# A graph network's edge lists, late node tiles and last normalizings, put in another order

## The chip, the cores and the metric

The kernel runs on one core of a Trainium2 chip. The metric is the device time of one execution in microseconds (us). The engines named below are TensorE (PE, its weight loads PEld), VectorE (DVE), ScalarE (ACT), GpSimd (POOL) and SyncE (SP). "SPq", "ACTq" and the like are the DMA queues that an engine issues to. L12 is line 12 of the kernel before.

## The reference, cut to what matters

There are 12,500 nodes of 128 features and 400,000 edges, sorted by destination.

```python
rbf = exp(-(distances[:, None] - centers) ** 2 / (2.0 * width * width))       # 50 centers, 0 to 10
cut = 0.5 * (cos(pi * distances / 10.0) + 1.0) * (distances <= 10.0)
W = (silu(rbf @ fw1 + fb1) @ fw2 + fb2) * cut[:, None]
messages = (h[src] @ pw + pb) * W
agg = segment_sum(messages, dst, 12500)
gnn = h + (silu(agg @ mw1 + mb1) @ mw2 + mb2)
x = layernorm(x + gnn)                                                        # h is x
```

Distances are drawn up to some 56, so most edges lie past the cutoff of 10 and add nothing.

## The kernel before, in words

**Edges.** Edges past the cutoff are dropped on the chip. The edge list is taken in seven chunks. For each, `load_rows` brings lengths, sources and destinations into SBUF, and `pack(c)` (L693) moves the edges that stay together: passes of shifts on DVE, by one, two, four places and so on (L515, L519, L509), then places within the whole from sums on PE (L729, read by DVE at L503), then a scatter to DRAM (`packed`) that GpSimd issues. `unpack(c)` (L811) reads the packed list back: loads of three lists by SP (L821), merged by DVE (`one_of`, L839 and L840, and two more operations to L869), transposed by PE (L902, in `to_places`, L899) and copied by DVE (L907) into `srci` (the source of each edge, by which rows are gathered). Between the transposes and that copy stands `lengths`, a merge of the edge lengths and their stores by SP. Then the same for `dl` (place within a window of destinations) and `cut` (the cutoff's factor); `at_row` (L921) holds addresses for rows that are copied singly.

The packed edges make 139 quads (`NL`) of 512 edges, four to each partition. The third chunk (c = 2) holds quads 24 to 45.

**A planner's order.** `pack` and `unpack` are generators: each `yield` gives the estimated time of what was recorded, and adds to an estimated clock. `pack_until` takes the next step of the first chunk whose due time `awake[c]` is not ahead of that clock; a chunk whose loaded lists haven't been taken into use (`c in sent`) goes first. `awake[c]` is set where a step has to wait for something: after the list's loads (L831) and, by `later`, between PE's transposes and the copies behind them (L906). The order in which instructions are recorded is the order in which each engine runs them, so a due time moves DVE, PE, SP and GpSimd work against the quads' work. The gathers (`fetch`) are recorded as far ahead as the lists are known and buffers are free.

**Quads.** For each quad q the main loop (L1489 to L1550) records:

- `fetch`: four indirect gathers on GpSimd (L1048), one row of `proj` (x @ pw + pb) for each partition. For eight quads the first of the four is replaced by single rows that SP copies. Each gather also waits for a sum some quads back (`FOLLOW`, "keeps pace with the sums"; L1051).
- `radial`, `basis`, `first`, `silu`, for two quads at a time: lengths by DMA, Square and Exp on ACT (L1094, L1095), PE by fw1 (L1103), Silu on ACT (L1109). `second`: PE adds fb2 (L1117) and multiplies by fw2 (L1120).
- `message`: DVE multiplies by the gathered rows (L1131); `place`: DVE makes the columns that hold cut at the destination's place (L1143); `sum_up`: PE sums over the edges (L1163) into one or two windows of destinations; `add`: DVE adds these to `aggT` (L1196).

Exp, Silu and the root (Sqrt) stand in different tables of ACT; a change from one to the other shows as ACT_TABLE_LOAD.

**Nodes.** From quad 70 on, `nodes(q)` (L1296) and `tail(q)` (L1337) take blocks of node tiles (128 nodes each) as their sums are complete: `node_first` (L1200; PE at L1204 and L1205, Silu on ACT), `node_second` (PE), `node_stats` (L1219; residual and statistics on DVE), `deviations` (L1232; four small operations on DVE, the last at L1240, and the root on ACT, L1241), `scales` (L1244; reciprocal at L1248 and L1249 on DVE), `normalize` (L1255; ACT at L1263, or DVE at L1260, then the store, L173). The early blocks, of four tiles, have one root for four blocks. The late ones begin at tiles 80 (4 tiles), 84 (4), 88 (2), 90 (3), 93 (2) and 95 (3, behind the last quad).

What touches the change near the end: the roots of the last early blocks and of tile 80 are recorded at quads 133 and 132 (`nodes` and L1532, `NL` - 6 and `NL` - 7), the latter followed by a Silu of one element (`warm`), which loads silu's table again. The last pair of quads' `silu` is recorded at quad 133 behind the first of these. At quad 133 `tail` records `keep_busy(8)` (L1342), eight products on PE into the bank `ph` that serve nothing (L1352), ahead of `node_first(84)`. Two more of them stand at each of the last quads (L1510). At the end, behind the last quad, stand `deviations([95])` and then the normalizings of tiles 90 to 92, 93 and 94 on ACT, `scales` of 95 to 97, and their normalizing, two on DVE and one on ACT.

```python
1051            if table is None and idx is None and len(last_sum) > FOLLOW:
1052                tc.add_manual_dep(ins.ins, last_sum[-1 - FOLLOW], mybir.DependencyInfo(
```

Of the kernel before, what the change touches and what calls it, by code (L numbers as in the profile page):

```python
# [43 lines left out]
NL = 139  # L44
# [39 lines left out]
def kernel(  # L84
# [37 lines left out]
    nc = tc.nc  # L122
# [215 lines left out]
    srci = keep.tile([P, NP, 2], I32, name="srci")  # L338
# [61 lines left out]
    clock = [3.2]  # L400
# [3 lines left out]
    awake = [0.0] * NC_  # L404
# [406 lines left out]
    def unpack(c):  # L811
# [15 lines left out]
        if c < 2:  # L827
            more_ = np_ if c == 0 else SPILL
            also = work.tile([P, 2, QE], F32, name="s", bufs=3).bitcast(I32)
            listed(also, 0, more_, 3, LISTS)  # L830
        awake[c] = max(awake[c], clock[0]) + (6 if c < 1 else 3.5 if c < 2 else 4.0)  # L831
        yield 0
        def alike_in(k):
            nc.vector.tensor_tensor(pair[:more_, :LISTS - 3, k::2], pair[:more_, :LISTS - 3, k::2],
# [46 lines left out]
        def later(more=0.0):  # L881

            if c or known[0] >= DIRECT // QT:
                awake[c] = clock[0] + (5.0 if known[0] >= QB[c + 1] else 1.0 if c == 0 else 2.5) + more
                return 0.0
            return 0.5
# [12 lines left out]
        def to_places(f, to):  # L899
            t, tp = turned()  # L900
            for j in range(2):
                nc.tensor.transpose(tp[:, j, :np_], f[:, j * P:(j + 1) * P], ident[:np_, :np_])  # L902
            if to is srci:
                lengths()
                yield 1.4 if c < 2 else 0.8
            yield later(-2.0 if c == 1 and to is srci else 0.0)  # L906
            nc.vector.tensor_copy(to[:, p0:p0 + np_, :].rearrange("p r j -> p j r"),  # L907
                                  tp[:, :, :np_])
            back(t)
# [288 lines left out]
    zs_of, py_of, st_of = {}, {}, {}  # L1198
# [20 lines left out]
    def node_stats(t0, st, between=lambda: None):  # L1219

        r = rows(t0)
        y, b = x_sb[t0], py_of.pop(t0)
        py = b.rearrange("p (k f) -> p k f", k=4)
        for a, c, m in alike(r):
            nc.vector.scalar_tensor_tensor(y[:m, a:a + c], y[:m, a:a + c], 2.0, py[:m, a:a + c],
                                           op0=OP.mult, op1=OP.add)
        free.append(b)
        between()
        for k, m in enumerate(r):
            nc.vector.bn_stats(st[:m, k, :], y[:m, k, :])  # L1230
# [13 lines left out]
    def scales(group, both, s):  # L1244

        n = s.shape[1]
        r, by = (work.tile([P, 16], F32, name=k, bufs=2)[:, :n] for k in ("rs", "by"))
        nc.vector.reciprocal(r, s)  # L1248
        nc.vector.scalar_tensor_tensor(by, both[:, :, 0], -0.5, r, op0=OP.mult, op1=OP.mult)  # L1249
        at = 0  # L1250
        for t in group:
            ready.append((t, r[:, at:], by[:, at:]))
            at += len(rows(t))

    def normalize(t0, rs, by, on=(), eng=nc.sync):  # L1255

        y = x_sb.pop(t0)
        for k, m in enumerate(rows(t0)):
            if k in on:
                nc.vector.tensor_scalar(y[:m, k, :], y[:m, k, :], rs[:m, k:k + 1], by[:m, k:k + 1],  # L1260
                                        op0=OP.mult, op1=OP.add)
            else:
                nc.scalar.activation(y[:m, k, :], y[:m, k, :], AF.Identity, bias=by[:m, k:k + 1],  # L1263
                                     scale=rs[:m, k:k + 1])
        node_dma(t0, y, out, True, eng=eng)

    ready = []
# [18 lines left out]
    begin, at_q = {}, NODES  # L1286
# [4 lines left out]
        begin[t0] = [at_q, at_q + 1, at_q + (4 if NODES + 24 < at_q < NL - 20 else 3)]  # L1291
        at_q += 2 if at_q % 4 == 1 else 3
    early = list(begin)
    assert begin[early[-1]][2] <= NL - 3

    def nodes(q):  # L1296

        if deep:
            scales(*deep.pop())
        for _ in ready[:1 if q < NL - 6 else 2]:  # L1300
            normalize(*ready.pop(0))
        for k, t0 in enumerate(early):
            if begin[t0][0] - 5 == q:
                load_x(t0)
            if begin[t0][2] == q:
                if k % 4 == 0:
                    st_of[0] = statistics()
                node_stats(t0, st_of[0][:, k % 4 * 4:])
                if k % 4 == 3:
                    deep.append(deviations(early[k // 4 * 4:k + 1], st_of[0]))  # L1310
            if begin[t0][1] == q:
                node_second(t0)
            if begin[t0][0] == q:
                node_first(t0)
        for k, t0 in enumerate(TAIL):
            if q == NL - 9 + k:
                load_x(t0)
        if q == NL - 7:
            st_of[3] = statistics()
            node_stats(80, st_of[3])  # L1320
        if q == NL - 4:
            node_stats(84, st_of[3][:, 4:])
        if q == NL - 3:
            node_stats(88, st_of[3][:, 8:])
            dev_of.append(deviations([84, 88], st_of[3][:, 4:]))
            nc.scalar.activation(warm, half_pi, AF.Silu)
        if q == NL - 2:
            node_second(90)
            for k in (1, 2):
                st_of[k] = statistics()  # L1330
            scales(*dev_of.pop(0))
            for _ in (84, 88):
                normalize(*ready.pop(0))
# [3 lines left out]
    def tail(q):  # L1337

        for t0, k in READY.items():
            if q == NL - k:  # L1340
                if t0 == 84:
                    keep_busy(8)  # L1342
                assert done_to(2 * added(q + 1)) >= (t0 + TAIL[t0]) * P
                node_first(t0)
            if q == NL - k + 1 and t0 in (80, 84, 88):
                node_second(t0)

    def keep_busy(n):

        ph = ps.tile([P, 2, QE], F32, name="ph", bufs=1)  # L1350
        for k in range(n):
            nc.tensor.matmul(ph[:, k % 2, :], ones_b[:, :P],  # L1352
                             bias_b["mb2"].rearrange("k j f -> k (j f)"), start=True, stop=True)
# [135 lines left out]
    for q in range(NL - 1):  # L1489
        while todo and q + 2 >= DIRECT // QT and todo[0] <= chunk_of(min(q + 2, NQ - 1)):  # L1490
            go_on(todo[0])
        msg = message(q)
        if q == NL - 2:
            bases_of(q, NL)
        nodes(q)
        most[0] = room(q)
        fetches(clock[0], most[0])
        fetches(math.inf, min(NL, q + AHEAD + 1))
        assert fetched[0] > QT * min(NL - 1, q + AHEAD)
        if q >= CLEAR_Q:  # L1500
            clear()
        if loads_later and q >= 8:
            nc.sync.dma_start(*loads_later.pop(0))
        radials(q // 2 + 5)
        one_by_one()
        multiplies(q + 1 + EARLY_X)
        if q + 2 < NL:
            second(q + 2)
        if q % 4 < 2 and 2 * octs(q) < NL:
            first(octs(q))  # L1510
            silu(octs(q))
        if q % 4 == 3:
            for o in (q // 4 * 2 + 4, q // 4 * 2 + 5):
                if 2 * o < NL:
                    basis(o)
        if q > NL - 5:
            keep_busy(2)
        sum_up(q, msg)
        now = range(added(q), added(q + 1))
        for k in now if q < NL - 2 else ():  # L1520
            base_of(k, (0,))
        if q < NL - 2:
            place(q + 1)
        if q == NL - 4:
            place(NL - 1)
        if q == NL - 2:
            for j in range(QT):
                sum_up(NL - 1, message(NL - 1, (j, j + 1)), (j,))
        for k in now:
            if q < NL - 2:  # L1530
                base_of(k, (1,))
            if q == NL - 7 and k == now[0]:  # L1532
                deep.append(deviations([80], st_of[3]))
                nc.scalar.activation(warm, half_pi, AF.Silu)
            add(k)
        tail(q)
        clock[0] = max(clock[0], there_at[q])
        summed[q] = clock[0] + 0.7
        clock[0] += 2.2 + 0.3 * (windows(q) - 1)
        if q == 0:  # L1540
            clear_packed(2, nc.sync)
        if todo:
            pack_until(max(there_at[q + 1], clock[0] + (PACK_US if known[0] >= QB[3] else EARLY_US)), NC_)
        if NODES - 8 <= q < NODES - 2:
            part_of(*(("mb1", mb1_f) if q < NODES - 5 else ("mb2", mb2_f)), (q - NODES + 8) % 3)
        if not todo and not counted:
            counted.append(q)
            count()
        elif counted and some is None and fetched[0] >= QT * NL:
            some = nc.values_load(bad_i[0:1, 2:3], min_val=0, max_val=3 * E)  # L1550
# [9 lines left out]
    node_second(95)  # L1560
    early_dev = deviations([90, 93], st_of[1])
    node_stats(95, st_of[2], lambda: scales(*early_dev))
    last_dev = deviations([95], st_of[2])
    for _ in (90, 93):
        normalize(*ready.pop(0))
    scales(*last_dev)
    normalize(*ready.pop(0), on=(0, 1), eng=nc.scalar)

# [110 lines left out]
```

## Time and profile before

| | |
|---|---|
| time, median of 3 runs | 734.89 us (734.77 to 734.94) |
| the profiled execution | 736.03 us |
| its span in the trace | 734.3 us |
| granted clock of PE, mean | 0.92 |
| PE busy | 590.7 us (80%) |
| DVE busy | 560.2 us (76%) |
| GpSimd busy | 533.5 us (73%) |
| ACT busy | 403.0 us (55%) |
| DMA, mean | 124 GB/s |

A line of the page's groups or of the trace's views names the line of the kernel, the engine, the operation, and output <- inputs by the program's names, with the shapes. "x3" is the number of instructions. A bracket gives the engine's idle time ahead of the instruction and what released it. A name can be that of another use of the same buffer, since buffers are shared: a message may be called `msg` or `quad`. The granted clock is the share of full speed that PE was allowed.

### The profile page before, as it was taken

The numbers are of one execution on the slowest core, as the hardware profiler recorded it, in microseconds if no ns is written. First come the engines' busy times: TensorE is split into PE (matmuls) and PEld (weight loads), VectorE is DVE, ScalarE is ACT, GpSimd is POOL, SyncE is SP. The second block draws the span as 40 slices with busy tenths as digits, with TensorE's granted clock in tenths as the row PEclk, the third lists the DMA queues.
The fourth block names the chain that finished last, engine by engine and source line by source line (L and its number), as shares of the span: only waits on it lengthen the run. The fifth ranks groups of instructions, "written<-read, shape, count | busy, mean of one in ns | idle before, by whom it ended". The sixth has DMA issues, their size and how long they took to land.

```text
span 734.3 us, 13663 instructions
## 1 busy us (share of the span) xinstructions
PE 590.7 (80%) x3527; PEld 461.9 (63%) x3527; DVE 560.2 (76%) x1737; ACT 403.0 (55%) x574; POOL 533.5 (73%) x569
## 2 busy tenths in 40 slices
PE   6877876797888787878698969999978787778684
PEld 5766565676666665667476758777656565565463
DVE  8899798878878997989889957877455555556663
ACT  6557634274444864536457256859456644653763
POOL 7777777577777777777777777777777777777750
PEclk9999687999999998989989989999998999999886
DMA  8995442233234323343233343535333433343231
GB/s 267 313 318 189 143 128 73 89 120 99 76 110 128 95 85 101 99 127 88 83 111 113 96 134 97 155 120 151 110 113 94 127 124 98 98 142 116 79 114 53
DMA packets 53103, 91.37 MB, mean 124 GB/s; under 512 B 13824, under 2 KB 20576, under 8 KB 53018
## 3 DMA queue, kind: packets, MB, share of 16 engines
q1 hardware_dynamic: 34466, 53.20, 21.8%
q0 software_dynamic: 17840, 36.77, 18.1%
q8 instruction: 29, 0.48, 0.3%
q10 hardware_dynamic: 712, 0.46, 0.2%
q14 instruction: 56, 0.46, 0.2%
HBM read 74.59 MB, written 15.79 MB: 123 GB/s over the span
## 4 chain that ended last, share of the span: by engine, by line
DMA 13%; PE 13%; DVE 11%; POOL 9%; issue 6%; ACT 3%; DVEq 1%; POOLq 0%; SPq 0%; ACTq 0%
DMA quad<-proj,srci 11%; POOL quad L1048 9%; PE ph L1103 3%; PE bank L1120 3%; PE sums L1163 3%; DVE hot L1143 2%; DVE quad L1143 2%; PE bank L1205 1%; DVE msg L1131 1%; DMA pair<-packed 1%; DVE aggT L1196 1%; DVE st L1230 1%; DVEq L1173 1%; ACT x L1263 1%; DMA packed<-line,at_i 1%
## 5 line engine op out<-in xcount | busy, mean ns | idle before, releaser
L1048 POOL DMA_INDIRECT quad<-proj,srci x421 | 400.9, 952 | 132.5 <-issue 94.9
L1120 PEld LDWEIGHTS bank<-fw_sb,s 128*128 128x128 f32 x1112 | 159.7, 207 | 72.9 <-issue 65.8
L1109 ACT ACTIVATE s<-ph 128x1024 f32<-128x1024 f32 x70 | 71.2, 1017 | 179.7 <-PE ph L1103 179.5
L1120 PE MATMUL bank<-fw_sb,s 128*128 128x128 f32 x1112 | 159.7, 291 | 0.0
L1103 PE MATMUL ph<-rbf,w_sb 102*128 102x512 f32 x278 | 145.9, 651 | 6.7 <-ACT s L1109 3.5
L1163 PEld LDWEIGHTS sums<-hot,msg 128*128 128x128 f32 x816 | 107.6, 198 | 55.9 <-issue 27.5
L1143 DVE TENSOR_SCALAR hot<-iota_n,dl,cut 128x80 f32<-128x80 f32 (+4 forms) x408 | 109.1, 341 | 27.5 <-PE sums L1163 25.3
L1163 PE MATMUL sums<-hot,msg 128*128 128x80 f32 (+4 forms) x816 | 110.4, 280 | 14.2 <-DVE msg L1131 13.9
L1117 PE MATMUL bank<-fb_b,ones_b 96*128 96x512 bf16 x139 | 56.5, 406 | 54.8 <-DVE msg L1131 34.1
L1048 POOL DMA_INDIRECT x<-proj,srci x79 | 75.5, 955 | 24.2 <-issue 19.8
L1131 DVE TENSOR_TENSOR msg<-bank,quad 128x512 f32<-128x512 f32 (+1 forms) x82 | 55.5, 677 | 45.9 <-DMA quad<-proj,srci 41.6
L1103 PEld LDWEIGHTS ph<-rbf,w_sb 102*128 102x128 f32 x278 | 52.6, 211 | 46.1 <-issue 38.3
L1196 DVE TENSOR_TENSOR aggT<-aggT,sums 128x80 f32 (+4 forms) x209 | 53.9, 258 | 32.4 <-PE sums L1163 11.1
L1094 ACT ACTIVATE rbf<-d,rbf_bias,rbf_scale 102x512 f32<-102x512 f32 x70 | 56.3, 804 | 19.6 <-DMA d<-near_d 19.6
L1048 POOL DMA_INDIRECT quad<-in_x_dram,srci x48 | 46.7, 974 | 15.7 <-issue 11.9
L334 PEld LDWEIGHTS bank<-pw_sb,xT 128*128 128x128 f32 (+1 forms) x292 | 43.0, 212 | 9.4 <-issue 6.0
L1109 ACT ACT_TABLE_LOAD x36 | 46.2, 1283 | 0.6
L1095 ACT ACT_TABLE_LOAD x35 | 44.9, 1283 | 0.6
L1095 ACT ACTIVATE rbf<-rbf 102x512 f32<-102x512 f32 x70 | 44.1, 630 | 1.5
L334 PE MATMUL bank<-pw_sb,xT 128*128 128x128 f32 (+1 forms) x292 | 43.3, 296 | 0.7 <-ACT xT L984 0.6
L1163 PE MATMUL sums<-quad,quad 128*128 128x128 f32 (+3 forms) x296 | 40.8, 284 | 2.9 <-DVE quad L1131 2.8
L1143 DVE TENSOR_SCALAR quad<-iota_n,dl,cut 128x128 f32<-128x128 f32 (+3 forms) x148 | 40.6, 353 | 3.3 <-issue 2.1
(272 smaller groups left out, 791.4 us busy)
## 6 DMA issues: line engine op xcount, KB each, us to landing
d<-near_d SPq DMA_DIRECT2D x70, 256.0 KB
dl<-proj SPq DMA_DIRECT2D x1024, 0.5 KB
x<-in_x_dram SPq DMA_DIRECT2D x46, 256.0 KB
quad<-proj,srci POOLq DMA_INDIRECT x421
proj<-hp SPq DMA_DIRECT2D x24, 256.0 KB
out_dram<-x SPq DMA_DIRECT2D x22, 256.0 KB
r_d<-in_edge_weight_dram SPq DMA_DIRECT2D x5, 256.0 KB
r_dst<-in_dst_dram SPq DMA_DIRECT2D x5, 256.0 KB
```

Of the source, the lines that this page charges most:

```text
L334: nc.tensor.matmul(to[:m, k, :], lT[:, k * P:k * P + m], w, start=False, stop=(k == a + c - 1))
L1048: ins = nc.gpsimd.indirect_dma_start(out=got[:, j, :], out_offset=None, in_=proj if table is None else table, in_offset=bass.IndirectOffse ...
L1094: nc.scalar.activation(rbf[:u], d[:u], AF.Square, bias=rbf_bias[:u], scale=rbf_scale[:u])
L1095: nc.scalar.activation(rbf[:u], rbf[:u], AF.Exp, scale=-1.0 / (2.0 * width * width))
L1103: nc.tensor.matmul(ph[:, h, :], w1_sb[:2 * KR, h, :], rbf[:2 * KR], start=True, stop=True)
L1109: nc.scalar.activation(s[:, :n], ph[:, :n], AF.Silu)
L1117: nc.tensor.matmul(pu, ones_b[:, :P], bias_b["fb2"].rearrange("k j f -> k (j f)"), start=True, stop=False)
L1120: nc.tensor.matmul(pu[:, j * H:(j + 1) * H], s[:, j * P:(j + 1) * P], fw2_sb, start=False, stop=(j == QT - 1))
L1131: nc.vector.tensor_mul(msg[:, a:b, :], pu_of[q].rearrange("p (j f) -> p j f", j=QT)[:, a:b, :], got_of[q][:, a:b, :])
L1143: nc.vector.tensor_scalar(hot[:, j, :wide(q)], iota_n[:, :wide(q)], dl[:, at[0], at[1]], cut[:, at[0], at[1]], op0=OP.is_equal, op1=OP.mult)
L1163: ins = nc.tensor.matmul(pa[:, k * W:k * W + wide(q)], msg[:, j, :], hot[:, j, :wide(q)], start=(j % n == 0), stop=(j % n == n - 1))
L1196: nc.vector.tensor_add(to, to, pa[:, k * W:k * W + wide(q)])
```

## The change

It has three parts.

1. The third chunk's lists. After their loads (L831) the due time of chunk 2 is set to the estimated clock itself instead of 4.0 us later, and the copy of its `srci` (L906) is due 2.5 us sooner behind PE's transposes. The merges are thus recorded right behind the loads.
2. The late roots. The root of the last early blocks is not recorded in `nodes` at quad 133 any more, but within that quad's additions (L1532), directly ahead of tile 80's, which moves there from quad 132; both stand behind the last `silu` of the quads. `nodes` takes all waiting groups in `scales` at quad 134, the older first. The eight fillers ahead of `node_first(84)` go. An assertion now says that the last early block ends at quad 133.
3. The end. `normalize` takes an argument for the engine of its first kind of normalizing. Tiles 90 to 92 are normalized on GpSimd, 93 and 94 on ACT, and both are recorded ahead of the last root, `deviations([95])`.

```diff
--- before.py
+++ after.py
@@ -828,7 +828,7 @@
             more_ = np_ if c == 0 else SPILL
             also = work.tile([P, 2, QE], F32, name="s", bufs=3).bitcast(I32)
             listed(also, 0, more_, 3, LISTS)
-        awake[c] = max(awake[c], clock[0]) + (6 if c < 1 else 3.5 if c < 2 else 4.0)
+        awake[c] = max(awake[c], clock[0]) + (6 if c < 1 else 3.5 if c < 2 else 0.0 if c < 3 else 4.0)
         yield 0
         def alike_in(k):
             nc.vector.tensor_tensor(pair[:more_, :LISTS - 3, k::2], pair[:more_, :LISTS - 3, k::2],
@@ -903,7 +903,7 @@
             if to is srci:
                 lengths()
                 yield 1.4 if c < 2 else 0.8
-            yield later(-2.0 if c == 1 and to is srci else 0.0)
+            yield later((0.0, -2.0, -2.5, *4 * (0.0,))[c] if to is srci else 0.0)
             nc.vector.tensor_copy(to[:, p0:p0 + np_, :].rearrange("p r j -> p j r"),
                                   tp[:, :, :np_])
             back(t)
@@ -1252,12 +1252,12 @@
             ready.append((t, r[:, at:], by[:, at:]))
             at += len(rows(t))
 
-    def normalize(t0, rs, by, on=(), eng=nc.sync):
+    def normalize(t0, rs, by, on=(), eng=nc.sync, v=nc.vector):
 
         y = x_sb.pop(t0)
         for k, m in enumerate(rows(t0)):
             if k in on:
-                nc.vector.tensor_scalar(y[:m, k, :], y[:m, k, :], rs[:m, k:k + 1], by[:m, k:k + 1],
+                v.tensor_scalar(y[:m, k, :], y[:m, k, :], rs[:m, k:k + 1], by[:m, k:k + 1],
                                         op0=OP.mult, op1=OP.add)
             else:
                 nc.scalar.activation(y[:m, k, :], y[:m, k, :], AF.Identity, bias=by[:m, k:k + 1],
@@ -1291,12 +1291,12 @@
         begin[t0] = [at_q, at_q + 1, at_q + (4 if NODES + 24 < at_q < NL - 20 else 3)]
         at_q += 2 if at_q % 4 == 1 else 3
     early = list(begin)
-    assert begin[early[-1]][2] <= NL - 3
+    assert begin[early[-1]][2] == NL - 6
 
     def nodes(q):
 
-        if deep:
-            scales(*deep.pop())
+        while deep:
+            scales(*deep.pop(0))
         for _ in ready[:1 if q < NL - 6 else 2]:
             normalize(*ready.pop(0))
         for k, t0 in enumerate(early):
@@ -1306,7 +1306,7 @@
                 if k % 4 == 0:
                     st_of[0] = statistics()
                 node_stats(t0, st_of[0][:, k % 4 * 4:])
-                if k % 4 == 3:
+                if k % 4 == 3 and q != NL - 6:
                     deep.append(deviations(early[k // 4 * 4:k + 1], st_of[0]))
             if begin[t0][1] == q:
                 node_second(t0)
@@ -1338,8 +1338,6 @@
 
         for t0, k in READY.items():
             if q == NL - k:
-                if t0 == 84:
-                    keep_busy(8)
                 assert done_to(2 * added(q + 1)) >= (t0 + TAIL[t0]) * P
                 node_first(t0)
             if q == NL - k + 1 and t0 in (80, 84, 88):
@@ -1529,7 +1527,8 @@
         for k in now:
             if q < NL - 2:
                 base_of(k, (1,))
-            if q == NL - 7 and k == now[0]:
+            if q == NL - 6 and k == now[0]:
+                deep.append(deviations(early[-4:], st_of[0]))
                 deep.append(deviations([80], st_of[3]))
                 nc.scalar.activation(warm, half_pi, AF.Silu)
             add(k)
@@ -1560,9 +1559,9 @@
     node_second(95)
     early_dev = deviations([90, 93], st_of[1])
     node_stats(95, st_of[2], lambda: scales(*early_dev))
+    normalize(*ready.pop(0), on=(0, 1, 2), v=nc.gpsimd)
+    normalize(*ready.pop(0))
     last_dev = deviations([95], st_of[2])
-    for _ in (90, 93):
-        normalize(*ready.pop(0))
     scales(*last_dev)
     normalize(*ready.pop(0), on=(0, 1), eng=nc.scalar)
```

## The prediction

> **What bounds the kernel now.** I read the page's groups first, then GpSimd's timeline, then the chain of waits, then the other engines where GpSimd stands.
>
> ```profile
> L1131 DVE TENSOR_TENSOR msg<-bank,quad 128x512 f32<-128x512 f32 (+1 forms) x82 | 55.5, 677 | 45.9 <-DMA quad<-proj,srci 41.6
> ```
>
> Behind the first bar stand busy time, mean ns of one, and the idle time before, with what ended most of it: VectorE's messages (L1131) wait above all for gathered rows. GpSimd gathers them (L1048), four gathers to a quad of 512 edges. In the timeline (start, length, and in brackets the idle time before and its releaser) one takes 0.95 us and the next starts 0.30 us later, so a quad costs 5.0 us. They stand back to back but for one hole, just ahead of quad 24, the first whose rows the third chunk's lists name:
>
> ```profile
> 130.54 1.00 POOL L1048 DMA_INDIRECT quad<-proj,srci  x1 [0.30 <-issue]
> 135.96 0.94 POOL L1048 DMA_INDIRECT quad<-proj,srci  x1 [4.42 <-DVE at_row L921]
> ...
> 680.02 0.94 POOL L1048 DMA_INDIRECT quad<-proj,srci  x1 [0.30 <-issue]
> ...
> 708.85 0.95 POOL L1048 DMA_INDIRECT quad<-proj,srci  x1 [0.30 <-issue]
> ```
>
> The last releaser named is at_row, but the built program has gather 24 wait for the copy of srci (L907), which starts at 135.44 and is the instruction ahead of at_row. The hole is worth 4.42 - 0.30 = 4.12 us.
>
> Does GpSimd set the end? The chain of waits holds this piece (start, length), the landing of quad 132's last gather:
>
> ```profile
> 680.02 2.48 DMA quad<-proj,srci
> ```
>
> So a gather lands 2.48 us after its start, and here the chain waits for that. Early on the gathers lead: near 130 GpSimd is at quad 24 and DVE (rows below) at message 5; near 488 it is at quad 94 and DVE at message 90, which is the least lead there is, and from then on messages wait for rows. At the end it is otherwise: the last gather, started at 708.85, lands at 711.33, yet the last message (below) starts only at 715.16. There the other engines are late. So two stages count: the hole near 131, if its gain survives to 488, and the stretch from 682 to the end.
>
> **Part 1, the third chunk's lists.** What stands now:
>
> ```profile
> 116.57 0.77 SPq L821 DMA_DIRECT2D pair<-packed  x2
> ...
> 200.43 0.79 SPq L821 DMA_DIRECT2D pair<-packed  x2
> ```
> ```profile
> 120.20 0.68 DVE L515 TENSOR_SCALAR bank<-nodes 128x512 int32<-128x512 int32 x1
> 125.27 0.22 DVE L503 TENSOR_SCALAR at_f<-bank,end 128x1 f32<-128x1 f32 x1 [2.28 <-PE bank L729]
> 127.73 0.67 DVE L1131 TENSOR_TENSOR msg<-bank,quad 128x512 f32<-128x512 f32 x1
> 129.87 0.41 DVE L839 TENSOR_TENSOR two<-pair 44x256 int32<-44x256 int32 x1
> 135.44 0.25 DVE L907 CAST srci<-bank 128x88 int32<-128x88 f32 x1 [0.43 <-PE bank L902]
> 204.34 0.42 DVE L839 TENSOR_TENSOR two<-pair 46x256 int32<-46x256 int32 x1 [0.53 <-DMA pair<-packed]
> ```
> ```profile
> 124.79 0.36 PE L729 MATMUL bank<-run,ones 128*128 128x1 f32 x2
> 156.75 1.00 PE L1163 MATMUL sums<-hot,msg 128*128 128x56 f32 x8
> ```
>
> In the new order the merge (L839 to L869, four operations, 1.5 us) stands right behind the L515 of 120.20, so at 120.9. Are the lists there? The next chunk's load was issued at 200.43 and its merge, which waited for it, ran at 204.34: 3.9 us. So this one is there at 120.5, 0.4 us ahead. Then come the rest of the first shifting pass (L519 and two L509, 2.0 us) and the lengths (0.85 us), to 125.2. PE's transposes (L902) now stand right behind the L729 of 124.79 and end near 125.4; the copy of srci ends near 125.9. Gather 24 may then start at 130.54 + 1.00 + 0.30 = 131.84, and the hole is gone: **-4.12 us**, bounds 0 and -4.4 (the whole idle time).
>
> What is behind the new waits: the message of quad 5 stands behind that copy at 125.6, 2.1 us ahead of its 127.73, since the wait of 2.28 us for L729 falls away (at_f now comes later). No arithmetic is added. SP's stores of the lengths and the row loads of single quads move with the list, the stores earlier by some 7 us; nothing but DVE's merge waits on SP here.
>
> What is late next? The built program lets each gather also wait for a sum (L1163) four quads back by the order of recording, and in the new order quads 24 to 33 wait for a sum one later. The tightest is the second gather of quad 28, the 17th behind that of 135.96 and so at 157.21 (17 x 1.25): it waits for sum 9, the row of 156.75, which ended at 157.75. Without the hole it comes to start at 153.1. If the sum did not move, the whole gain would be lost there. It does move: two whole passes of the fourth chunk's shifting (four operations of 0.7 us as that of 120.20, 2.8 us each) now stand behind message 9 instead of ahead of it. With 5.6 us less DVE work and 2.3 us less waiting ahead of it, against 1.5 to 3 us of new waits of DVE for sums (two buffers of one-hot columns turn round), sum 9 ends 4.9 to 6.5 us earlier, 151.2 to 152.9 by an estimate from these rows. It fits, with 0.2 to 1.9 us to spare.
>
> The next narrow place is where the lead runs out:
>
> ```profile
> 488.38 0.95 POOL L1048 DMA_INDIRECT quad<-proj,srci  x1 [0.32 <-issue]
> ```
> ```profile
> 436.07 0.42 DVE L839 TENSOR_TENSOR two<-pair 54x256 int32<-54x256 int32 x1 [7.17 <-DMA dl<-proj]
> 486.93 0.69 DVE L1131 TENSOR_TENSOR quad<-bank,quad 128x512 f32<-128x512 f32 x1
> ```
>
> Quad 94 is gathered into the buffer that message 90 reads until 487.62, 0.76 us before the gather's start. With GpSimd 4.12 us ahead, message 90 must come 3.4 us earlier. It can: ahead of it DVE stands 7.17 us for the last chunk's lists, and the new order puts that merge behind message 79 instead of 77. Its scatter, one quad of gathers later but 4.12 us ahead, gives the lists at 436.07 + 5.0 - 4.12 = 436.95; two messages are then done during the wait, which puts message 80 where 78 was, plus 0.9 us. That is some 7 us earlier from there on. So I keep 4.12.
>
> **Part 2, both roots behind the last silu, no fillers.**
>
> ```profile
> 687.44 1.28 ACT L1241 ACT_TABLE_LOAD   x1
> 693.72 1.28 ACT L1109 ACT_TABLE_LOAD   x1
> 695.02 0.60 ACT L1109 ACTIVATE s<-ph 128x512 f32<-128x512 f32 x1
> 711.88 1.28 ACT L1241 ACT_TABLE_LOAD   x1 [2.82 <-DVE v L1240]
> ```
> ```profile
> 689.07 0.18 DVE L1248 RECIPROCAL rs<-dev 128x4 f32<-128x4 f32 x1 [1.00 <-ACT dev L1241]
> 692.86 0.61 DVE L1196 TENSOR_TENSOR aggT<-aggT,sums 128x128 f32 x2
> 715.16 0.88 DVE L1131 TENSOR_TENSOR quad<-bank,quad 128x128 f32<-128x128 f32 x4
> ```
> ```profile
> 695.66 3.57 PE L1352 MATMUL ph<-mb_b,ones_b 96*128 96x512 bf16 x8 [5.54 <-ACT s L1109]
> 699.46 1.91 PE L1205 MATMUL bank<-aggT,mw_sb 128*128 128x512 f32 x2
> 702.86 1.06 PE L1163 MATMUL sums<-quad,quad 128*128 128x128 f32 x8
> 713.75 0.91 PE L1205 MATMUL bank<-aggT,mw_sb 128*128 128x384 f32 x2 [1.95 <-DVE aggT L1196]
> 718.91 1.31 PE L1163 MATMUL sums<-quad,quad 128*128 128x128 f32 x8
> ```
>
> Now ACT loads the root's table (687.44), silu's, the root's again and silu's (693.72), and only then runs the last silu at 695.02; the eight fillers need the bank that it reads, PE stands 5.54 us, and L1205 of tile 84 waits behind them until 699.46. In the new order the last silu follows the one ahead of 687.44 directly, one pair of loads (2 x 1.28) is gone, and L1205 waits for DVE's sums alone. DVE's stall of 1.00 us and the two operations behind it (0.3 us) leave the place ahead of those sums; tile 80's four small ones only move within it. So the sums run at 692.86 - 1.3 = 691.6 and end at 692.2. L1205 starts there instead of at 699.46: -7.3 us. If each instruction behind it keeps its length (L1205 to sum 134 is 3.40 us), the chain to the end moves by **-7.3 us**. Tile 80's four normalizings (1.63 us, as the four of 726.77 below) go to where ACT is idle 2.82 us, ahead of 711.88; without that cover they would cost their 1.6 us. Its store goes from the head of SP's late stores to behind four others, and two loads behind those come with the stores that they follow, earlier like the rest.
>
> The rows bound this. The last gather lands at 711.33; a quarter message (0.22) and a quarter sum (0.33) later the last sum ends at 711.9, against 720.2 now (718.91 + 1.31): at most -8.3. The bound on the other side comes from the clock. These rows have the stretch, its length, PE busy, the granted clock, DMA share and GB/s:
>
> ```profile
> 695.00:701.00 6.00, 5.33 (x11) 0.50 0.25 75
> 701.00:703.00 2.00, 2.00 (x12) 0.66 0.15 43
> 716.00:720.00 4.00, 4.00 (x22) 0.57 0.29 102
> ```
>
> Behind the gap of 5.54 us the clock is 0.50 and comes back near 702, some 6 us after the fillers start. If it falls as far behind the new gap, the work itself must fill those 6 us from 692.2 on; its 3.40 us are as slow as now, and 2.6 us more run at 0.50, which costs 1.3: -6.0. But the new gap, from where the old wait began (695.66 - 5.54 = 690.1) to 692.2, is 2.1 us. The nearest row for it is the last: 0.57, behind a gap of 1.95 us (row of 713.75). So I keep the slow lengths and no more. The Trainium skill, "TensorE: Matmul & The Clock Gate", Part 1, says that PE falls to half clock after an idle window of about 3.4 us and needs as much busy time to return; by that the new gap leaves the clock full, and part 2 would come to the bound of -8.3. The rows behind 5.54 us agree with it; the row of 716 to 720 speaks against it.
>
> **Part 3, GpSimd normalizes three tiles.**
>
> ```profile
> 1.02 0.29 POOL masks.py:199 TENSOR_SCALAR_AFFINE_SELECT ident<-ident 128x128 f32<-128x128 f32 x1
> ```
> ```profile
> 725.14 0.17 DVE L1249 SCALAR_TENSOR_TENSOR by<-both_m,rs 128x5 f32<-128x5 f32 x1
> 727.31 0.60 DVE L1260 TENSOR_SCALAR x<-x,rs,by 128x128 f32<-128x128 f32 x2
> 726.77 1.63 ACT L1263 ACTIVATE x<-x,by,rs 128x128 f32<-128x128 f32 x4
> 728.04 1.16 SPq L173 DMA_DIRECT2D out_dram<-x  x2
> 729.20 0.58 ACTq L173 DMA_DIRECT2D out_dram<-x  x1
> ```
>
> ACT's six normalizings, from 726.77 on, end the chain, and the last store leaves at 729.20. Three go to GpSimd, two go ahead of the last root, one is left behind it: at 727.3, when DVE has its scales, plus 0.4 (1.63 / 4). Its store is second in ACT's queue, behind the one that waits for DVE's two (727.91) and takes 0.4 us, and so leaves at 728.35: **-0.85 us**. GpSimd starts at 725.4 (725.14 + 0.17); no row shows this operation on it. One costs between 0.29 (the nearest row, of the same size) and 0.95 us (a gather): three end at 726.3 to 728.3, and SP's second store, 0.6 us behind the first, leaves by 728.9. Bounds -0.85 and -0.3; I take the near row.
>
> **Sum.** The profiled execution took 736.03 us, 1.7 of them outside its span of 734.3, and 1.14 more than the median 734.89. Its span becomes 734.3 - 4.1 - 7.3 - 0.8 = 722.1, it 723.8, and with the same 12.2 off the median: **722.7 us**.
>
> **Rivals.**
> 1. *The pace waits take part 1.* Sum 9 and its neighbours come no earlier, GpSimd stands behind them, and what it loses it never regains. For: the reserve is 0.2 us at one end of the estimate. Against: less DVE work ahead of them. Gain 8.1: 726.8 us; half lost, 724.8. Chance 0.22.
> 2. *The clock stays full behind the short gap*, until the last gather binds. Parts 1 and 3 as above, -8.3 in part 2: 721.7 us. Chance 0.17.
> 3. *The low clock lasts longer, the fillers being gone.* Part 2 -6.0: 724.0 us. Chance 0.10.
> 4. *Slower: the lists land late.* DVE stands at the merge at 120.9, behind it message 5, PE's transposes, all sums, and GpSimd by its pace waits, microsecond for microsecond. Part 1's 4.1 and the 8.1 of the others are eaten from a landing about 12.5 us late (133.4) on; at 15 us late 737 us. Only the 3.9 us of 200.43 speaks against it. Chance 0.05.
> 5. *The merge does not close the hole*, because the copy still waits on PE behind other work; as rival 1, 726.8 us. Chance 0.03.
>
> **How the numbers follow.** The forecast, 722.7, has 0.43, with its own range 721.5 to 724. The range 721.0 to 727.8 takes in rivals 1, 2, 3 and 5, and leaves out the slower one and both of the first and third together. A difference of 0.2% (1.5 us) is about what a measurement tells from none: all cases but rival 4 lie past it. Faster 0.93, same 0.02, slower 0.05.
>
> **What would show it.** Right: no idle time above 0.4 us on GpSimd from 131 to 709; srci copied near 125.8; last gather started near 704.7; the wait for the last chunk's lists under 6 us; L1205 of tile 84 within 10.5 us of the landing of quad 132; no L1350 filler between sum 133 and it; the last store under 2 us behind the last root. Wrong: GpSimd idle ahead of quads 25 to 30 or 86 to 95 on PE or DVE (rival 1), or a gap of PE above 3 us between sums 133 and 134. The forecast falls as a whole if the gathers do not set messages 100 to 132.

## The result, and the profile after

| | before | after |
|---|---|---|
| median, 4 runs of each | 734.91 us (734.77 to 735.37) | 723.20 us (723.02 to 724.27) |
| ratio to before | | 0.9843, 95% interval 0.9826 to 0.9860 |
| profiled execution, its span | 736.03, 734.3 us | 723.36, 721.6 us |
| mean granted clock of PE | 0.92 | 0.91 |

The changed kernel takes 11.7 us less; 12.2 were forecast. In the profiled executions it is 12.7, and that sum can be taken apart by stage. GpSimd's timeline of the changed kernel (start, length, idle time before and its releaser):

```profile
132.79 0.94 POOL L1048 DMA_INDIRECT quad<-proj,srci  x1 [0.30 <-issue]
...
154.06 0.98 POOL L1048 DMA_INDIRECT quad<-proj,srci  x1 [0.31 <-DVE msg L1131]
...
704.88 0.94 POOL L1048 DMA_INDIRECT quad<-proj,srci  x1 [0.30 <-issue]
713.90 1.32 POOL L1260 TENSOR_SCALAR x<-x,rs,by 128x128 f32<-128x128 f32 x3 [8.08 <-ACT dev L1241]
```

132.79 is the counterpart of 135.96: the hole of 4.42 us ahead of quad 24 is gone, no idle time above 0.31 us stands between it and the last gather, and that one starts 3.97 us earlier (708.85 before). VectorE's timeline:

```profile
123.32 0.41 DVE L839 TENSOR_TENSOR two<-pair 44x256 int32<-44x256 int32 x1
127.73 0.25 DVE L907 CAST srci<-bank 128x88 int32<-128x88 f32 x1 [0.19 <-PE bank L902]
...
358.54 0.42 DVE L839 TENSOR_TENSOR two<-pair 46x256 int32<-46x256 int32 x1 [7.61 <-DMA pair<-packed]
435.92 0.42 DVE L839 TENSOR_TENSOR two<-pair 54x256 int32<-54x256 int32 x1 [2.09 <-DMA pair<-packed]
438.92 0.68 DVE L1131 TENSOR_TENSOR msg<-bank,quad 128x512 f32<-128x512 f32 x1
...
707.47 0.29 DVE L1131 TENSOR_TENSOR quad<-bank,quad 128x128 f32<-128x128 f32 x1 [1.06 <-DMA quad<-proj,srci]
```

The third chunk's merge doesn't wait, and its list is copied by 127.98, 4.8 us ahead of the gather of 132.79. The last quarter message now waits for the last gather (704.88 and the 2.48 us of a landing give 707.36, it starts at 707.47), which it did not before. TensorE and ScalarE at the end:

```profile
685.17 1.05 PE L1163 MATMUL sums<-hot,msg 128*128 128x128 f32 x8
687.85 1.13 PE L1205 MATMUL bank<-aggT,mw_sb 128*128 128x512 f32 x2 [1.40 <-DVE aggT L1196]
689.92 1.06 PE L1163 MATMUL sums<-quad,quad 128*128 128x128 f32 x8
702.34 0.91 PE L1205 MATMUL bank<-aggT,mw_sb 128*128 128x384 f32 x2 [2.29 <-DVE aggT L1196]
705.64 1.91 PE L1163 MATMUL sums<-hot,msg 128*128 128x128 f32 x8
707.35 1.28 PE L1163 MATMUL sums<-quad,quad 128*128 128x128 f32 x8
```
```profile
685.37 0.60 ACT L1109 ACTIVATE s<-ph 128x512 f32<-128x512 f32 x1 [1.84 <-PE ph L1103]
685.99 1.28 ACT L1241 ACT_TABLE_LOAD   x1
715.13 0.30 ACT L1241 ACTIVATE dev<-v,eps 128x3 f32<-128x3 f32 x1 [0.50 <-DVE v L1240]
716.50 1.06 ACTq L173 DMA_DIRECT2D out_dram<-x  x2
```

The last silu runs ahead of the root's table load, and L1205 of tile 84 waits for the additions alone. The last sum ends at 708.63 (707.35 + 1.28) instead of 720.22, 11.6 us earlier: 4.0 from the gathers and 7.6 from the tail. From there to the end of the span it is 13.0 us instead of 14.1, the 1.1 of part 3. The three add up to 12.7. How the clock was granted to TensorE (stretch, length, PE busy with the number of instructions, clock, DMA share, GB/s), in stretches that the last section explains:

```profile
683.92:687.33 3.41, 2.52 (x16) 1.00 0.21 58
...
697.57:700.99 3.42, 1.97 (x13) 1.00 0.81 244
700.99:704.40 3.41, 1.65 (x8) 1.00 0.25 63
704.40:707.81 3.41, 3.41 (x17) 0.50 0.39 130
```

Between sums 133 and 134 the clock was full this time.

### The profile page after: what moved, and what is told of

Same layout as the page of the kernel before. It is cut to its first block, busy times and chain, and to the rows that moved or that the text cites. A ratio compares the mean times of both kernels' runs of the same rounds, so it can differ in the third digit from the quotient of the medians.

```text
span 721.6 us, 13649 instructions
## 1 busy us (share of the span) xinstructions
PE 588.0 (81%) x3519; PEld 462.7 (64%) x3519; DVE 560.8 (78%) x1737; ACT 399.6 (55%) x569; POOL 534.3 (74%) x572
## 4 chain that ended last, share of the span: by engine, by line
DVE 30%; PE 24%; DMA 14%; issue 13%; POOL 11%; ACT 4%; DVEq 2%; SPq 0%; ACTq 0%; POOLq 0%
POOL quad L1048 11%; DMA quad<-proj,srci 9%; PE ph L1103 7%; DVE hot L1143 5%; PE bank L1120 5%; PE sums L1163 5%; DVE msg L1131 3%; PE bank L334 3%; DVE aggT L1196 2%; DVE r_d L509 2%; DVE bank L515 2%; DVEq L1173 2%; PE bank L1117 2%; DVE nodes L519 2%; DVE quad L1143 1%
## 5 line engine op out<-in xcount | busy, mean ns | idle before, releaser
L1163 PEld LDWEIGHTS sums<-hot,msg 128*128 128x128 f32 x816 | 109.5, 200 | 57.7 <-issue 27.6
L1196 DVE TENSOR_TENSOR aggT<-aggT,sums 128x80 f32 (+4 forms) x209 | 53.7, 257 | 30.9 <-PE bank L1205 11.7
L1131 DVE TENSOR_TENSOR quad<-bank,quad 128x512 f32<-128x512 f32 (+2 forms) x40 | 25.3, 632 | 25.6 <-DMA quad<-proj,srci 21.6
```

The lines of the kernel that those rows point to most:

```text
L1131: nc.vector.tensor_mul(msg[:, a:b, :], pu_of[q].rearrange("p (j f) -> p j f", j=QT)[:, a:b, :], got_of[q][:, a:b, :])
L1163: ins = nc.tensor.matmul(pa[:, k * W:k * W + wide(q)], msg[:, j, :], hot[:, j, :wide(q)], start=(j % n == 0), stop=(j % n == n - 1))
L1196: nc.vector.tensor_add(to, to, pa[:, k * W:k * W + wide(q)])
```

## The experiments

All edits are against the kernel before or the changed one, as said. They ran in three sets, each on a chip of its own; each ratio is to runs of the kernel before on the same chip.

**The three parts, each alone**, on a chip where the kernel before took 735.91 us (732.32 to 741.17, 25 runs). Their edits are the parts of the diff above.

Part 1: 

> The kernel before with part 1 alone. Theory (gathers set the messages up to quad 132, and the tail hangs on message 132): the hole ahead of quad 24 is gone, the last gather starts 4.0 us earlier (near 704.9 of the span), everything behind quad 132 moves with it, 730.9 us (-4.0). Rival (pace waits or the tail's own limits take the gain): the gathers lose it again behind GpSimd waits of over 0.4 us, or the last sum stays near 720; 733 us or more.

730.97 us, ratio 0.9921 (0.9895 to 0.9946), so 4.0 to 7.7 us. By the traces GpSimd has no idle time above 0.4 us from 120 us to the last gather. That one starts at 705.26, against 708.02, 708.27 and 709.37 in the three kernels beside it, which lack part 1. Part 3 alone is the one of them whose tail is the old one up to the last sum: against it the last gather starts 4.1 us earlier (709.37) and the last sum ends 3.8 us earlier (716.77, 720.52). So the tail moved with the gathers. The theory holds.

Part 2: 

> The kernel before with part 2 alone. Theory (with the PE stall gone the tail runs into the landing of the last gather, 711.33): the last message starts within 0.3 us of that landing, the last sum ends near 712.6 instead of 720.2, 727.3 us (-7.6). Rival (PE's slow clock behind the gap keeps the chain at -7.3 of its own, as the prediction had it): about the same time, but the last message starts 0.5 us or more behind the landing, and the granted clock between sums 133 and 134 is under 0.7. Rival of additivity (part 2 needs part 1): under -5 us, over 730.

728.22 us, ratio 0.9893 (0.9830 to 0.9956). The last gather starts at 708.02 and the last message at 710.50, right at its landing (708.02 + 2.48); sum 134 starts 2.07 us behind L1205 of tile 84, where it was 3.40 before. The theory holds and the prediction's own reading falls: the tail doesn't stop at -7.3 on a slow clock, it runs on until the gather binds. Part 2 needs no part 1.

Part 3: 

> The kernel before with part 3 alone. Theory: -0.85 to -1.1 us, 733.8 to 734.1; GpSimd takes about 0.44 us for a tile and the last store leaves under 2 us behind the last root. Rival (the stores of the queue set the end, not the normalizings): no change, 734.6 to 735.2.

735.52 us, ratio 0.9988 (0.9954 to 1.0022): by the time alone, neither theory. From the end of the last sum to the end of the span it is 12.9 us (733.4 - 720.52), as in the changed kernel and 1.2 under the kernel before; in the three traces beside it, which lack part 3, it is 14.1 to 14.3. So the traces side with the first. The three ratios multiply to 0.980; the changed kernel had 0.9843 and, on the next chip, 0.9805.

**Which half of part 2.** Only the fillers go:

```diff
-                if t0 == 84:
-                    keep_busy(8)
```

> The kernel before with only the eight fillers ahead of L1205 of tile 84 taken out; both roots stay where they were. Theory A (the cost was the fillers' wait for the bank that the last silu reads, with L1205 queued behind them on PE): L1205 of tile 84 starts near 693.5 instead of 699.46, -6 to -7.3 us, 727.6 to 729. Theory B (the cost was ACT's four table loads ahead of the last silu, and that silu is needed soon after by itself): PE goes on to wait for the silu of 695.0, gain under 2 us, over 733.

729.14 us, ratio 0.9905 (0.9876 to 0.9934), nearly all of part 2. TensorE's timeline of this kernel, and of part 3 alone, which has fillers and roots as before:

```profile
688.50 1.06 PE L1163 MATMUL sums<-hot,msg 128*128 128x128 f32 x8
692.96 1.13 PE L1205 MATMUL bank<-aggT,mw_sb 128*128 128x512 f32 x2 [3.18 <-DVE aggT L1196]
```
```profile
689.90 1.05 PE L1163 MATMUL sums<-hot,msg 128*128 128x128 f32 x8
696.50 3.57 PE L1352 MATMUL ph<-mb_b,ones_b 96*128 96x512 bf16 x8 [5.55 <-ACT s L1109]
700.29 1.87 PE L1205 MATMUL bank<-aggT,mw_sb 128*128 128x512 f32 x2
```

From sum 133 to L1205 of tile 84 it takes 10.4 us with both, 4.5 without the fillers and 2.7 without fillers and with the roots moved (part 2 alone and the whole change agree). So theory A: taking out the fillers, the instruction queued in front, saves 5.9 of these 7.7 us, and moving the roots as well another 1.8. That is the split for this order of the two edits only.

The other way round, roots moved and fillers kept, was run in the last set:

> The kernel before with both roots moved behind the last silu, and the eight fillers left where they were. Theory (the fillers cost only while they wait for the bank that the last silu reads; with that silu 4 us earlier they fit into the gap of PE): L1205 of tile 84 starts 0.3 to 0.6 us later than with both edits, which the wait for the last gather hides, so -7 to -8 us against the kernel before, the same as part 2 whole. Rival (the fillers cost their own 1.9 to 3.6 us): -4 to -6 us, and the last message starts over 1 us behind its landing.

That chip gives no time that can be used: the kernel before took 1029 us on it (1014 to 1040) and the changed one 1012. The waits of the changed kernel there, in total, times and longest:

```profile
POOL quad L1048 <- issue: 173.0, 398, 13.1
ACT s L1109 <- remote: 129.2, 15, 16.2
PEld bank L1120 <- issue: 114.7, 66, 21.8
```

Engines stand up to 22 us at a time for nothing that the profile names, so what sets the time there need not be what sets it on a quiet chip. The order of things near the end can still be read in TensorE's timeline. With the roots moved the fillers run right behind sum 133, without a wait:

```profile
978.07 1.92 PE L1163 MATMUL sums<-hot,msg 128*128 128x128 f32 x8
979.78 2.09 PE L1352 MATMUL ph<-mb_b,ones_b 96*128 96x512 bf16 x8
981.71 0.38 PE L1204 MATMUL bank<-ones_b,mb_b 96*128 96x512 bf16 x1
981.92 1.02 PE L1205 MATMUL bank<-aggT,mw_sb 128*128 128x512 f32 x2
```

L1205 starts 3.9 us behind the start of sum 133, and 2.6 in the changed kernel on that chip: the fillers cost 1.2 us there, more than the 0.3 to 0.6 expected and under the rival's 1.9. Whether the last gather hides that on a quiet chip wasn't shown. But moving the roots alone also takes away most of the wait: 3.9 us where the kernels with roots and fillers as before have 10.4 on the quiet chip (the kernel before has no trace on this one). Fillers and late silu made the wait together, and either edit removes most of it. The ratio, 0.9930 (0.9884 to 0.9977), says only that this kernel too is faster than the one before.

The yardstick of that set, and part 1 without its second half:

> The changed kernel a third time, as the yardstick for the runs beside it: 722.5 to 723.5 us; 18.5 us from the start of the last gather to the end, as in both runs so far.

> The changed kernel without the second half of part 1: the merge of the third chunk right behind its loads, but the copy of its source list not due 2.5 us sooner. Theory (the copy had 4 us to spare): it moves behind message 5 and its columns, to 130.3 or so, which is still ahead of 131.5, so no idle time of GpSimd over 0.5 us there and 722.5 to 723.5 us, as the changed kernel. Rival (both halves are needed): a hole of 1 to 4 us ahead of quad 24 and as much more time.

1012.3 us (ratio 0.9889) and 1017.23 us (0.9944, interval 0.9905 to 0.9983). In the second the copy of the list stands behind message 5, and GpSimd idles 6.29 us ahead of quad 24 (in the slowest of its executions, the profiled one), against 3.44 with both halves. With stalls of that size all around this settles neither theory; it stays open.

**Can the tail be had shorter?** Four runs on another chip (kernel before: 737.53 us, 734.4 to 742.21). The yardstick:

> The changed kernel once more, as the yardstick for the three runs beside it: 723.2 us on a chip on which the kernel before takes 734.9, so a ratio of 0.984 to the kernel before; last gather 4.0 us ahead of 708.85, last message within 0.2 us of its landing.

722.61 us, ratio 0.9805 (0.9771 to 0.9839); last gather at 703.61, last message at 706.21.

Eight fillers in the gap of 2.29 us ahead of L1205 of tile 90:

```diff
         for t0, k in READY.items():
             if q == NL - k:
+                if t0 == 90:
+                    keep_busy(8)
```

> The changed kernel with eight fillers on PE (1.9 us) in its gap of 2.29 us ahead of L1205 of tile 90. Theory (the granted clock of a stretch of some 3.3 us follows how busy PE was in the stretch before it): the clock from 704 to 708 is 1.0 instead of 0.57, the sum of quad 137 takes 1.06 us instead of 1.91, and since its addition stands behind the last gather's message anyway the time gains only 0.2 to 0.4 us: 722.9. Rival 1 (the clock falls for another reason): 0.57 as before, 723.2. Rival 2 (the low clock was on the path): -1 us or more.

724.21 us, ratio 0.9826, in the medians 1.6 us slower than the yardstick, which no theory expected. The clock did what the theory says; sum 137 took 1.05 us. But in the chain of waits of this kernel (first row) the last gather took 3.53 us to land, not 2.48, and then the clock fell one stretch later:

```profile
703.11 3.53 DMA quad<-proj,srci
```
```profile
700.95:704.37 3.42, 3.00 (x21) 1.00 0.22 58
704.37:707.78 3.41, 1.60 (x10) 1.00 0.42 139
707.78:711.19 3.41, 2.99 (x9) 0.50 0.01 2
```

TensorE waits for that landing, is busy 1.60 of 3.41 us, and all of the last blocks' products run at 0.50. What was won ahead of the gather was paid behind it.

The same fillers, and the addition of quad 137 with L1205 of tile 93 ahead of the last message:

```diff
             for j in range(QT):
+                if j == QT - 1:
+                    add(NL - 2)
+                    tail(q)
                 sum_up(NL - 1, message(NL - 1, (j, j + 1)), (j,))
...
-        tail(q)
+        if q < NL - 2:
+            tail(q)
```

> The same fillers, and the addition of quad 137 with L1205 of tile 93 recorded ahead of the last gather's message and sum. Theory (after the last landing the chain is last sum, its addition, L1205 of tile 95, and it now waits for L1205 of tile 93): L1205 of tile 95 starts near 709.1 instead of 709.88, -0.8 us against the changed kernel, 722.4. Rival (the last sum now stands behind L1205 of tile 93 on PE and comes that much later): 723.2 or more.

724.20 us (722.66 to 727.35), ratio 0.9832: the last sum was not late behind L1205 of tile 93, and from the last landing to the end of the span it takes 13.1 us instead of 14.2 in the changed kernel. But again the gather landed late:

```profile
704.21 3.62 DMA quad<-proj,srci
```

The late landing loses what the order wins. That is the profiled execution, which took 722.71 us; why the median lies 1.5 us higher isn't shown. I suspected the stores of tiles 84 and 88, which leave within 2.1 us of the gather's start; holding them behind the last sum, on top of that order:

```diff
+            for t0, y in late_out:
+                late = node_dma(t0, y, out, True)
+                tc.add_manual_dep(late.ins, last_sum[-1], mybir.DependencyInfo(
...
-                normalize(*ready.pop(0))
+                normalize(*ready.pop(0), put=False)
```

> The changed kernel with the eight fillers in the gap ahead of L1205 of tile 90, the addition of quad 137 and L1205 of tile 93 ahead of the last gather's message, and the stores of tiles 84 and 88 held behind the last sum. Theory (those stores collide with the last gather, which landed 3.5 and 3.6 us after its start in the two runs with fillers instead of 2.5): it lands 2.5 us after its start, from there to the end of the span as in order_fill 13.1 us, so 17.3 us from its start to the end instead of 18.5, 1.1 us under the yardstick. Rival (the late landing has another cause): 3.5 us again, and no gain over the yardstick. Rival 2 (the held stores end later than the last ones): SP's last store leaves behind ACT's.

This fell into the set on the stalling chip: 1012.59 us, ratio 0.9855 (0.9787 to 0.9924), not apart from its yardstick's 0.9889. The last gather started at 981.11, 16 us ahead of the last message, so the collision wasn't tested. Against it speaks that in the changed kernel the first of those stores leaves 0.98 us behind the last gather's start, and in gap_fill 0.94, and only the latter landed late.

The kept traces point to another cause. A landing is told by sixteen updates of a semaphore. In gap_fill and order_fill fifteen of them come 2.2 to 2.5 us after the gather's start, as in the changed kernel, and only the sixteenth at 3.53 and 3.62. In both, and in none of the other eight traces from quiet chips, one packet of a queue that the profile calls "instruction" (16 KB) runs while the last gather lands, from 1.40 us behind the gather's start for 1.08 us and from 1.57 us for 0.92. This is the row of gap_fill's DMA queues from 704.4 to 705.7 (packets, MB, share of 16 engines):

```profile
q8 instruction: 1, 0.02, 5.2%
```

In the changed kernel that packet comes 4.6 us behind the gather's start. One comes about every 250 instructions of TensorE in these traces, so eight products more with their weight loads, ahead of it, fit with its coming earlier. That it held up the DMA engine which carried the sixteenth part of the gather is inferred; the trace doesn't tell the engine. A collision with stores is another matter, and not excluded elsewhere: in the kernel before and with part 1 or part 3 alone, where nothing waits for the last gather, all sixteen updates come late, the last at 3.3 to 3.5 us, amid more of other transfers.

Last, a gather fewer:

```diff
-SINGLY = (22, 45, 62, 67, 86, 102, 118, 133)
+SINGLY = (22, 45, 62, 67, 86, 102, 118, 125, 133)
-A_ROW = .58
+A_ROW = .5
```

> The changed kernel with a ninth quad (125) whose first 128 rows SP copies singly, and the single rows paced at 0.50 instead of 0.58 us: one gather of GpSimd fewer. Theory (GpSimd's back-to-back gathers set the end): the last gather starts 1.25 us earlier, near 703.6, and the time is 722.0 (-1.25). Rival (the tail has hit PE and ACT as well): -0.4 or less. Rival (SP's rows come late or slow the gathers): 723.2 or more, with DVE waiting for quad 125 or 133.

726.55 us, ratio 0.9844: 3.9 us behind the yardstick, by the third case, though at another place. SP's timeline ahead of the last chunk's lists, and VectorE and GpSimd behind it:

```profile
426.13 5.86 SPq L1038 DMA_DIRECT2D dl<-proj  x16
...
436.45 0.71 SPq L821 DMA_DIRECT2D pair<-packed  x2
```
```profile
441.13 0.42 DVE L839 TENSOR_TENSOR two<-pair 54x256 int32<-54x256 int32 x1 [4.43 <-DMA pair<-packed]
```
```profile
445.59 0.95 POOL L1048 DMA_INDIRECT quad<-proj,srci  x1 [1.52 <-issue]
456.32 0.94 POOL L1048 DMA_INDIRECT quad<-proj,srci  x1 [2.26 <-PE ph L1103]
```

The loads of the lists (L821) leave at 436.45, 4.8 us later than in the changed kernel (431.63), with more single rows in SP's queue ahead of them; the merge follows at 441.13 instead of 435.92, GpSimd gets holes (the two longest behind the merge are shown), and the last gather starts at 706.47 rather than 703.6. No version here beats the changed kernel.

## Why the prediction came out as it did

- **What sets the time: right.** Two stages, the hole near 131 and the end. Part 1 alone moved the last gather and the last sum together. The landing at 711.33 was the gather's start and 2.48 us; by the semaphore's updates it came at 712.19, still 3.0 us ahead of the last message.
- **Part 1, -4.12: right, measured -3.97.** The lists were there, the merge didn't wait, and the pace held: sum 9 ended at 153.66 (152.66 + 1.00), the second gather of quad 28 started at 154.06, 0.40 us of reserve within the 0.2 to 1.9 of the estimate. Wrong was the place of the copy, 127.73 instead of 125.9: in this execution VectorE was 2.5 us late as early as message 2 (101.10 against 98.56), ahead of anything that the change moves. The copy kept 4.8 us to spare, so it cost nothing; in five more executions with part 1 it starts at 123.95 to 126.20. That 3.97 lies so near 4.12 is in part luck: ahead of quad 24 GpSimd was 1.00 us late too (131.54 against 130.54), so that quad's gather came only 3.17 us earlier, and gathers that were shorter on the way made up the other 0.80.
- **Where the lead runs out: right.** The last chunk's merge came at 435.92 (436.95 expected), with 2.09 us of waiting; message 80 moved from 446.09 to 438.92, the 7 us of the estimate. The chunk before now waits 7.61 us instead of 3.39, which I had not looked at; the lead was large enough there. Near 488, the narrow place, GpSimd doesn't stand still in the changed kernel, with part 1 alone, in gap_fill or in order_fill; how thin the lead is there shows with part 2 alone, where it stood 1.89 us (at 487.79).
- **Part 2, -7.3: the place right, the reason for the size wrong.** L1205 of tile 84 came at 687.85; 699.46 less 4.12 and 7.3 is 688.0. The step that failed is "So I keep the slow lengths": sum 134 followed after 2.07 us, not 3.40, on a full clock. Rival 2 took place, and the tail ran up to the last gather. It got 7.6, not the whole 8.3 that rival 2 gives. About 0.3 of the missing 0.7 is that a quarter message and a quarter sum that stand alone take longer than the 0.22 and 0.33 of the bound: 0.29 and 0.49 in gap_fill, on a full clock. Most of the rest goes, by that comparison, with a later stretch that was granted 0.50 (704.40 to 707.81), where the last two sums run. That 7.6 lies near the 7.3 forecast is luck: the errors almost cancel in the total.
- **Part 3, -0.85: right, measured -1.1.** A normalizing on GpSimd takes 0.44 us (1.32 / 3), between the bounds of 0.29 and 0.95, and nearer to the low one.
- **Rivals 1, 3, 4 and 5: no.** No pace wait held GpSimd, the low clock did not last longer behind sum 133, the lists were not late, the hole closed.
- **The sum.** 12.2 were forecast, 12.7 came in the profiled executions and 11.7 in the medians: the profiled run of before lay 1.1 us over its median, that of after 0.2, a difference that carrying the same 12.2 over could not see.

The two edits of part 2 were worked out as one; the run without the fillers shows that taking these out is enough for most of it.

## What to carry to other kernels

A filler that waits for a buffer is not free: what it costs is the wait of everything queued behind it on its engine, here 5.9 us for 1.9 us of work, and 1.2 us where the buffer was free. When one engine's hole is closed, follow its lead to the place where it is smallest before counting the gain, and take the landing of its last transfer as the floor of what the other engines can win at the end. Gains behind that floor came to nothing here: three further edits of the tail and of the queue that feeds it all lost at least as much as they won, two of them in the landing of the last gather itself.

## What the hardware showed that was not expected

The granted clock changes only at points of a fixed grid. In the changed kernel the edges from 438 us on are, read from windows of 0.5 us, at 438.16, 444.98, 547.38, 557.62, 584.93, 704.40 and 707.81 among others: all apart by whole multiples of 3.413 us. The grid lies elsewhere in each execution. Cut along its grid, the kernel before reads (columns as above):

```profile
685.30:688.72 3.42, 3.42 (x22) 1.00 0.23 60
688.72:692.13 3.41, 1.40 (x10) 1.00 0.20 58
692.13:695.54 3.41, 0.00 (x0) 0.50 0.60 178
...
712.61:716.02 3.41, 1.68 (x8) 1.00 0.00 0
716.02:719.44 3.42, 3.42 (x17) 0.50 0.34 120
```

A stretch in which TensorE is busy less than about half (1.40 and 1.68 of 3.41 us here, 1.65 in the changed kernel, 1.60 above) is followed by one at 0.50; 1.97 left the clock full. The border isn't sharp in these figures: in the changed kernel the stretch from 543.97 to 547.38, busy 1.84 us, was followed by 0.50, and the one from 656.62 to 660.03, busy 1.64 us, by a full clock. So it is not a gap's length or its end that decides, but mainly how much of it falls into one stretch. The gap of 1.95 us that I read as proof of a slow clock lay, with other idle time, in one stretch; the new gap shared its stretch with 2.52 us of work. With the same order and another grid the clock did fall there, in the run with the moved addition, and sum 134 followed L1205 of tile 84 after 3.64 us, no faster than the prediction had it:

```profile
684.47:687.88 3.41, 1.63 (x11) 1.00 0.23 58
687.88:691.29 3.41, 3.41 (x12) 0.50 0.24 58
```

The Trainium skill, "TensorE: Matmul & The Clock Gate", Part 1, says that the hardware watches a free-running window of 4096 cycles, some 3.4 us, and that cold matmuls vary from run to run with its phase. The grid agrees with that. Its rule names an idle window as what brings the half clock; here windows busy up to 1.84 of 3.41 us brought it too.

Not expected either: two last gathers that landed 3.5 and 3.6 us after their start, each while a 16 KB packet of the queue called "instruction" ran. The prediction's 2.48 is also not what every gather takes: of the 23 landings that stand in the changed kernel's chain of waits, 15 took 2.4 to 3.0 us and 8 took 3.1 to 3.7.
